# Layer 0 of a four-layer attention network: a set order for TensorE in the two first passes

## The chip, the cores and the metric

The kernel runs on one core of a Trainium2 chip. The metric is the device time of one execution in microseconds (us). In the text DVE is VectorE, ACT is ScalarE, POOL is GpSimd, SP is SyncE, and PE is TensorE; PEld is TensorE's weight load.

## The reference

The network takes x (8 batches, 256 tokens, 320 channels) and a context (8, 120, 192) through four layers. Only layer 0 is touched here. Its attention is quantised: queries, keys and values are rounded to 8-bit integers with one step for the whole tensor, which comes from the largest absolute value in it, and the softmax weights are rounded with a step from the largest weight in the whole tensor.

```
q = fq_sym(x @ Wq); k = fq_sym(ctx @ Wk); v = fq_sym(ctx @ Wv)
scores = einsum('bhnd,bhmd->bhnm', q, k) * dh ** (-0.5)
w = fq_zero(softmax(scores))
out = einsum('bhnm,bhmd->bhnd', w, v)   # then @ Wo + bo
```

with `fq_sym(x) = clip(round(x / d), -128, 127) * d`, `d = max|x| / 127`, and `fq_zero` the same with `d = max(x) / 255`. There are 20 heads of 16 channels. Layer 0 does this twice, first as self attention (keys are the 256 tokens) and then as cross attention (keys are the 120 context tokens), and ends in a feed-forward network. Layers 1 to 3 are attentions and feed-forward networks without rounding.

## The kernel before

Because the steps are maxima over everything, layer 0 goes over all eight batches several times. The class `Quant` (L1180) holds one attention; `s` is the self attention, `c` the cross attention.

*Projections.* `project_all` (L1207) makes queries, keys and values of the self attention batch by batch; ACT copies them from PSUM and `top` (L1201) takes the largest absolute value of each on DVE into a column of `am`. For the last batch the maxima of queries and keys are read from PSUM instead of from the copies. `keys_all` (L1259), `values_all` (L1273) and `queries_all` (L1284) do the same for the cross attention; there, too, the last batch's maxima of queries are read from PSUM, one for each third. `queries_all` has a table `at` of rounds in which a batch is normalised, transposed and projected; the last two batches are pulled together.

*Steps and rounding.* `steps` (L1319) reduces `am` over partitions and makes the steps. `whole(b)` (L1339) rounds: by adding a large number and taking it off again, the queries and keys of batch b become whole numbers in bf16, in five instructions: `tk` (L1347), `tq` (L1350), two halves of the keys (L1353 and L1357), and the queries (L1363 or L1365). They are on POOL, except that with `fast` the keys are on DVE and the last step of the queries is on ACT with a bias tile `magic`. `fast` is used for batch 0 of both attentions and for batch 1 of the cross attention.

*First pass.* It finds the sums of the softmax. A batch has 20 heads in five groups of four. A unit is, for the self attention, one group and half of its heads: 10 units a batch; for the cross attention two groups (or the last one) and half of their heads: 6 units a batch. For a unit there are three kinds of work, with the letters that the prediction uses:

- T, in `tops_all` (L1407): matmuls of the scores with tokens on the partitions (L1422), and a DVE reduction for the largest score of each token (L1425). When a batch is through, three DVE casts and two subtractions split its maxima into bf16 parts (`npx`, L1442 and L1444). In the third unit of the next batch TensorE transposes them (L1433) and ACT copies them to `nTs` (L1436).
- E, in `exps` (L1449): matmuls of the scores with keys on the partitions, and of `sel` with `nTs` to take the maxima off (both L1466), and ACT's exponential (L1473) into a tile `e` of a pool of five.
- S, in `add` inside `sums_all` (L1477): matmuls of `place` with `e` (L1488), which add up the exponentials over keys. When a batch is through, ACT copies its sums (L1493) and DVE takes their smallest (L1494).

T and E each take a pair of PSUM banks from one pool of three pairs, `ps_f`, in turn; so a tile of T or E waits until the reduction or exponential of the tile three before it has read its bank. S uses a pool of two banks, `ps_a`.

*What sets the order.* `weave` (L649) runs several of these generators round by round: in each round every generator whose start has come takes one step. That gives the program order. The order on each engine is then chosen by the framework's scheduler, which may bring an instruction ahead of others of its engine that are not ready in its model; it keeps data dependencies, and manual dependencies where the program adds them. For the self attention the parts are `tops_all` from round 0, `sums_all` (which calls `exps` first and then adds half of the units that wait) from round n + 4 with n = 10, `whole_all` (the rounding of batches 1 to 7) from round 0, and `keys_all` from round 7. The maxima of the cross keys are taken after it by a plain loop. For the cross attention the context's keys and values of later layers are made in the same weave: matmuls at L728, ACT copies to `kst` (L360, L364) and `vst` (L371, L372, L781), and stores to DRAM from SP.

*Second pass.* `weight_steps` (L1514) makes the step of the weights, and `out_all` computes the scores again, rounds the weights, multiplies by the values and projects. For the self attention `queries_all` of the cross attention is woven in from round 8, and three steps of `values_all` from round 5B + 1.

The main part calls these in order: `project_all`, `steps`, `whole(0)`, the weave of the first pass, the second pass, and the same for `c`.

Of the kernel before, what the change touches and what calls it, by code (L numbers as in the profile page):

```python
# [11 lines left out]
F32 = mybir.dt.float32  # L12
# [6 lines left out]
P = 128  # L19
# [35 lines left out]
class Kernel:  # L55
# [118 lines left out]
    def open_quant(self, pool):  # L174
# [8 lines left out]
        self.magic = pool.tile([P, 1], F32, name="magic")  # L183
        nc.gpsimd.memset(self.magic, -MAGIC)
# [94 lines left out]
    def weight_o2(self, pool, name):  # L279
# [8 lines left out]
        return w  # L288

# [274 lines left out]
    def ff_item(self, blk, ln, which, func, w, brow):  # L564
# [11 lines left out]
        def out():  # L576
# [5 lines left out]
            def mm(*args, **kw):  # L582
                nonlocal last
                ins = nc.tensor.matmul(*args, **kw)  # L584
                if last is not None:
                    order = mybir.DependencyInfo(mybir.DependencyClass.NoSync, mybir.DependencyReason.DATA)
                    self.tc.add_manual_dep(ins.ins, last.name, order, reason="order of the rows' forms")
                last = ins.ins
# [591 lines left out]
class Quant:  # L1180
# [5 lines left out]
    def __init__(self, k, pool, kpool, ln, w, brow, cross):  # L1186
# [8 lines left out]
        self.am = pool.tile([P, 3, B + 2], F32, name=f"am_{n}")  # L1195
        nc.gpsimd.memset(self.am, 0.0)
        self.sc = pool.tile([P, 16], F32, name=f"sc_{n}")
        self.q, self.kk, self.v = {}, {}, {}


    def top(self, i, b, src):  # L1201
        self.k.nc.vector.tensor_reduce(
            self.am[: src.shape[0], i, b : b + 1], src, AX.XY if len(src.shape) > 2 else AX.X, ALU.max,
            apply_absolute_value=True,
        )

    def project_all(self):  # L1207
# [11 lines left out]
        for b in range(B):  # L1219
# [29 lines left out]
            if b + 1 < B:  # L1249
                self.top(0, b, q)  # L1250
                self.top(1, b, kt)
                continue

            for i, ps in enumerate((pq, pk)):
                self.top(i, b, ps[:, :, :N])
            for i, ps in enumerate((pq, pk)):
                self.top(i, B, ps[:, i, N:])
# [26 lines left out]
    def queries_all(self):  # L1284
# [12 lines left out]
        def project(b, m):  # L1297
# [3 lines left out]
            if b + 1 == B:  # L1301
                self.top(0, b + m, ps[:, 0, :N])
            elif m == 2:
                self.top(0, b, self.q[b])

        at = {b: [5 * b + i for i in (0, 3, 6, 7, 8)] for b in range(B - 2)}
        at[B - 2] = [5 * B - 10 + i for i in (0, 3, 4, 5, 7)]
        at[B - 1] = [5 * B - 10 + i for i in (3, 6, 7, 8, 9)]  # L1310
        for r in range(5 * B):
            for b in range(B):
                for i, n in enumerate(at[b]):
                    if n == r:
                        norm(b) if i == 0 else turn(b) if i == 1 else project(b, i - 2)
            yield
# [22 lines left out]
    def whole(self, b, fast=False):  # L1339
# [7 lines left out]
        to.tensor_scalar(tk[:, : 3 * nk], kt, sc[:, 7:8], MAGIC, ALU.mult, ALU.add)  # L1347
        yield
        tq = k.work.tile([P, 3 * N], F32, tag="xh", name="tq")
        nc.gpsimd.tensor_scalar(tq, q, sc[:, 6:7], MAGIC, ALU.mult, ALU.add)  # L1350
# [11 lines left out]
        if fast:  # L1362
            nc.scalar.activation(qh.rearrange("p c n -> p (c n)"), tq, AF.Identity, bias=k.magic)  # L1363
        else:
            to.tensor_scalar(qh.rearrange("p c n -> p (c n)"), tq, MAGIC, None, ALU.subtract)  # L1365
# [24 lines left out]
    def whole_all(self):  # L1390

        for b in range(1, B):
            n = 0
            for _ in self.whole(b, self.cross and b == 1):
# [12 lines left out]
    def tops_all(self):  # L1407
# [3 lines left out]
        for b in range(B + 1):  # L1411
            if b < B:
                negm = k.small.tile([P, 4, G, TPB], F32, tag="negm", name="negm")
            for i, (gs, h) in enumerate(self.units):
                if b < B:
                    s = k.pair()
                    for n, g in enumerate(gs):
                        for t in range(TPB):
                            for j in range(2):
                                kt, q = self.operands(b, g, 2 * h + j)  # L1420
                                o = (n * TPB + t) * nk
                                nc.tensor.matmul(  # L1422
                                    s[:, j, o : o + nk], q[:, t * P : (t + 1) * P], kt, start=True, stop=True
                                )
                    nc.vector.tensor_reduce(  # L1425
# [23 lines left out]
    def exps(self, b, gs, heads, kind):  # L1449
# [5 lines left out]
        for shift in (False, True):  # L1455
            for i, g in enumerate(gs):
                for c in range(kc):
                    for at, j in enumerate(heads):
# [7 lines left out]
                        nc.tensor.matmul(  # L1466
# [9 lines left out]

    def sums_all(self):  # L1477

        k, nc, kc, ks = self.k, self.k.nc, self.kc, self.ks
        st, todo = {}, []  # L1480

        def add(b, g, c, es, at):
# [4 lines left out]
            for j in range(4):  # L1487
                nc.tensor.matmul(  # L1488
# [7 lines left out]
        es = []  # L1496
        for b in range(B):
            for gs, h in self.units:

                if h == 0:  # L1500
                    es = []
                    for _ in range(len(todo) - len(self.last) if todo else 0):
                        add(*todo.pop(0))
# [289 lines left out]
```

## Time and profile before

| | us |
|---|---|
| median of three runs | 2235.7 (2229.62 to 2238.51) |
| profiled execution, its own time | 2235.43 |
| profiled execution, span | 2233.4 |
| mean granted clock of TensorE | 0.965 of full speed |
| self projections end, first reduction of the self first pass | 103.9, 111.0 |
| end of the self first pass | about 258 |
| first T of the cross first pass, its end | 414.5, about 547 |

The profile is taken from one execution. Busy times are shares of its span; stretches are read in us from the span's start. The granted clock is the share of full speed that TensorE was allowed. The difference of 2.0 us between the profiled execution's own time and its span lies outside the first and last instruction. The places of the stages are read from the times at which the groups of lines named above begin and end.

### The profile page before, as it was taken

What the parts mean: (1) busy time and instruction counts of PE and PEld (TensorE: products, weight loads), DVE (VectorE), ACT (ScalarE), POOL (GpSimd) and SP (SyncE); (2) the same over time, 40 slices, a digit from 0 to 9 for tenths busy, and PEclk for the clock granted to TensorE, in tenths of its full rate; (3) what the DMA queues carried; (4) which work ended last, traced back from release to release, by engine and by line L of the source; (5) the groups of instructions that cost most, each with busy time, mean ns of one, the idle gap of its engine ahead of it and who ended that gap; (6) DMA issues with size and microseconds to landing.
All of it is one profiled execution on the core that took longest, in us unless ns stands there. A gap on an engine that the chain in (4) does not pass through costs nothing.

```text
span 2233.4 us, 38265 instructions
## 1 busy us (share of the span) xinstructions
PE 2044.5 (92%) x16413; PEld 1201.3 (54%) x16413; DVE 1117.4 (50%) x1698; ACT 825.7 (37%) x1252; POOL 357.9 (16%) x365
## 2 busy tenths in 40 slices
PE   6889878898899999999999999899999799999997
PEld 5643345554444555465555555554555455666664
DVE  4388677555752221335655667611121466556465
ACT  2347878467532121124444443411201233222221
POOL 1092066601411000000000001100000100000100
PEclk9989889898889999999999999999999899999999
DMA  4000000642110000020000001100000201000000
GB/s 117 17 12 2 1 1 4 167 111 57 55 53 28 1 0 1 1 92 2 2 2 22 27 25 35 47 1 0 1 1 2 68 25 32 12 24 26 23 19 16
DMA packets 79303, 63.21 MB, mean 28 GB/s; under 512 B 48410, under 2 KB 68318, under 8 KB 78622
## 3 DMA queue, kind: packets, MB, share of 16 engines
q1 hardware_dynamic: 75070, 57.06, 9.3%
q10 hardware_dynamic: 4064, 3.71, 0.6%
q8 instruction: 129, 2.11, 0.4%
q14 instruction: 40, 0.33, 0.1%
HBM read 42.61 MB, written 17.37 MB: 27 GB/s over the span
## 4 chain that ended last, share of the span: by engine, by line
PE 75%; DVE 16%; ACT 5%; issue 3%; DMA 1%; POOL 1%; SPq 0%; ACTq 0%; DVEq 0%; POOLq 0%
PE pf L120 13%; PE pf L584 13%; PE pf L132 9%; PE pa L120 7%; PE pa L447 6%; PE pf L430 4%; PE pa L584 3%; PE pf L139 3%; PE pf L385 3%; DVE negm L1425 3%; PE pf L1466 3%; PE pf L728 3%; DVE rs L455 2%; PE pa L1488 2%; DVE negm L392 2%
## 5 line engine op out<-in xcount | busy, mean ns | idle before, releaser
L436 ACT ACTIVATE e<-pf 128x1024 f32<-128x1024 f32 (+2 forms) x176 | 158.3, 944 | 234.9 <-PE pf L430 227.8
L392 DVE TENSOR_REDUCE negm<-pf 128x4 f32<-128x1024 f32 (+4 forms) x224 | 188.1, 886 | 108.8 <-PE pf L385 108.8
L584 PE MATMUL pf<-xTf,ff 128*128 128x512 f32 x512 | 232.4, 601 | 5.2 <-DVE negm L392 5.2
L455 DVE RECIPROCAL rs<-pa 128x256 f32<-128x256 f32 x88 | 152.2, 1745 | 144.0 <-PE pa L447 144.0
L477 POOL TENSOR_TENSOR xb<-x_sb,brow 128x640 f32<-128x640 f32 x40 | 62.2, 1555 | 792.2 <-DVE x_sb L483 748.2
L1473 ACT ACTIVATE e<-pf,sc_s 128x1024 f32<-128x1024 f32 x160 | 169.6, 1116 | 49.4 <-PE pf L1466 42.6
L1425 DVE TENSOR_REDUCE negm<-pf 128x4 f32<-128x1024 f32 (+2 forms) x128 | 143.3, 1134 | 68.1 <-PE pf L1422 61.4
L611 DVE SCALAR_TENSOR_TENSOR hT<-pf,cols_sb,gl 128x512 f32<-128x512 f32 x64 | 48.0, 751 | 256.8 <-ACT gl L610 254.5
L120 PE MATMUL pf<-ff,hT 128*128 128x320 f32 x640 | 174.4, 434 | 0.0
L584 PEld LDWEIGHTS pf<-xTf,ff 128*128 128x128 f32 x512 | 94.9, 191 | 125.2 <-issue 119.8
L120 PEld LDWEIGHTS pf<-ff,hT 128*128 128x128 f32 x640 | 120.9, 190 | 55.5 <-issue 6.1
L430 PE MATMUL pf<-qT,kT 32*128 32x256 f32 (+1 forms) x1280 | 122.3, 411 | 21.9 <-DMA qT<-nT 12.8
L610 ACT ACTIVATE gl<-pf,cols_sb 128x512 f32<-128x512 f32 x64 | 43.9, 687 | 248.0 <-PE pf L584 248.0
L385 PE MATMUL pf<-kT,qT 32*128 32x120 f32 (+1 forms) x1920 | 114.8, 329 | 18.3 <-ACT e L436 18.1
L120 PE MATMUL pa<-o,oT 128*128 128x320 f32 x352 | 105.4, 441 | 15.2 <-DVE oT L456 14.1
L385 PEld LDWEIGHTS pf<-kT,qT 32*128 32x128 f32 x1920 | 84.9, 189 | 58.4 <-ACT e L436 27.7
L1466 PE MATMUL pf<-Q,K 32*128 32x256 bf16 (+1 forms) x960 | 90.5, 294 | 25.3 <-DVE negm L1425 13.2
L639 POOL TENSOR_TENSOR xb<-x_sb,brow 128x640 f32<-128x640 f32 x16 | 25.1, 1566 | 543.1 <-DVE x_sb L644 528.7
L447 PE MATMUL pa<-e,v 128*32 128x256 f32 (+1 forms) x1280 | 105.2, 388 | 2.3 <-ACT e L436 1.7
L1581 DVE TENSOR_SCALAR w<-e 128x1024 bf16<-128x1024 f32 (+2 forms) x128 | 87.4, 691 | 37.5 <-ACT e L1473 36.3
L430 PEld LDWEIGHTS pf<-qT,kT 32*128 32x128 f32 (+1 forms) x1280 | 68.7, 183 | 68.3 <-issue 37.3
L132 PE MATMUL pf<-xT,q 128*128 128x256 f32 x384 | 101.0, 392 | 0.4 <-ACT e L436 0.2
(287 smaller groups left out, 3448.1 us busy)
## 6 DMA issues: line engine op xcount, KB each, us to landing
ff<-in_L_xattn_Wff_dram SPq DMA_DIRECT2D x1, 2560.0 KB
qT<-nT SPq DMA_DIRECT2D x160, 4.0 KB
ff<-in_L_xattn_ff_w_dram SPq DMA_DIRECT2D x1, 2560.0 KB
out_dram<-x_sb SPq DMA_DIRECT2D x16, 160.0 KB
kd_cross<-kst SPq DMA_DIRECT2D x8, 300.0 KB
vd_cross<-vst SPq DMA_DIRECT2D x8, 300.0 KB
vd_both<-vst SPq DMA_DIRECT2D x8, 300.0 KB
kT<-kd_cross SPq DMA_DIRECT2D x8, 300.0 KB
```

Of the source, the lines that this page charges most:

```text
L120: self.nc.tensor.matmul(out, l, r, start=i == 0, stop=i == len(pairs) - 1)
L132: self.nc.tensor.matmul(o, *t[c], start=start and c == 0, stop=stop and c == n - 1, skip_group_check=True)
L385: nc.tensor.matmul(s[j // 2][:, j % 2, o : o + nk], qT[r : r + PAD, g, t * P : (t + 1) * P], kT[r : r + PAD, g, :nk], start=True, stop=True,)
L392: nc.vector.tensor_reduce(negm[:, n, 2 * i : 2 * i + 2, g0 : g0 + len(gs), :].rearrange("p j g t -> p j (g t)"), sv[:, :, :, k0:k1], AX.X, ...
L430: nc.tensor.matmul(s[j // 2][:ks, j % 2, o : o + N], kT[r : r + PAD, g, c * ks : (c + 1) * ks], qT[r : r + PAD, g, :], start=True, stop=True,)
L436: nc.scalar.activation(e[:ks, 2 * i : 2 * i + 2, :n], s[i][:ks, :, :n], AF.Exp, scale=scale)
L447: nc.tensor.matmul(o[j * PAD : (j + 1) * PAD, what * N : (what + 1) * N], w, es[g][:ks, j, c * N : (c + 1) * N], start=first and c == 0 an ...
L455: nc.vector.reciprocal(rs, o[:, N:])
L584: ins = nc.tensor.matmul(*args, **kw)
L1425: nc.vector.tensor_reduce(negm[:, 2 * h : 2 * h + 2, gs[0] : gs[-1] + 1, :].rearrange("p j g t -> p j (g t)"), s[:, :, : len(gs) * TPB * n ...
L1466: nc.tensor.matmul(s[at // 2][:ks, at % 2, o : o + N], l, m, start=not shift and o == 0, stop=shift and o + N == n, skip_group_check=True,)
L1473: nc.scalar.activation(e[:ks, :, :n], ps[:ks, :, :n], AF.Exp, scale=self.sc[:ks, 9:10])
```

## The change

It has these parts.

1. A helper `behind` adds a dependency of order alone (no semaphore) between two instructions. `Quant.mm` chains with it all matmuls of T, E and S of an attention's first pass, in program order. The weave names E, T and S as three parts in that order, `exps_all` being split from `sums_all`; S now takes half of the waiting units in even rounds and all in odd ones.
2. In the self attention's weave, `keys_all` starts at round 2 instead of 7; the maxima of the cross keys are ordered behind the reduction of the last T.
3. The last batch's maxima are taken from the SBUF copies, as those of the others are.
4. `whole` with `fast` has `tk` on POOL and `tq`, both halves of the keys and the last step of the queries on DVE; ACT has no part and `magic` goes. Batch 1 of the cross attention is no longer `fast`.
5. `queries_all` has the same rounds for every batch, four more in all; the end of `out_all` has two more rounds and takes one unit from its list in each; the values start three rounds later.

```diff
+    def behind(self, ins, last, reason):
+        if last is not None:
+            order = mybir.DependencyInfo(mybir.DependencyClass.NoSync, mybir.DependencyReason.DATA)
+            self.tc.add_manual_dep(ins.ins, last.ins.name, order, reason=reason)
...
+    def mm(self, *args, **kw):
+        ins = self.k.nc.tensor.matmul(*args, **kw)
+        self.k.behind(ins, self.last_mm, "order of the rows' forms")
+        self.last_mm = ins
...
-            if b + 1 < B:
-                self.top(0, b, q)
-                self.top(1, b, kt)
-                continue
-            for i, ps in enumerate((pq, pk)):
-                self.top(i, b, ps[:, :, :N])
-            for i, ps in enumerate((pq, pk)):
-                self.top(i, B, ps[:, i, N:])
+            self.top(0, b, q)
+            self.top(1, b, kt)
...
-            if b + 1 == B:
-                self.top(0, b + m, ps[:, 0, :N])
-            elif m == 2:
+            if m == 2:
                 self.top(0, b, self.q[b])
-        at = {b: [5 * b + i for i in (0, 3, 6, 7, 8)] for b in range(B - 2)}
-        at[B - 2] = [5 * B - 10 + i for i in (0, 3, 4, 5, 7)]
-        at[B - 1] = [5 * B - 10 + i for i in (3, 6, 7, 8, 9)]
-        for r in range(5 * B):
+        todo = {0: norm, 3: turn, 6: lambda b: project(b, 0), 7: lambda b: project(b, 1), 8: lambda b: project(b, 2)}
+        for r in range(5 * B + 4):
...
-        to.tensor_scalar(tk[:, : 3 * nk], kt, sc[:, 7:8], MAGIC, ALU.mult, ALU.add)
+        nc.gpsimd.tensor_scalar(tk[:, : 3 * nk], kt, sc[:, 7:8], MAGIC, ALU.mult, ALU.add)
...
-        nc.gpsimd.tensor_scalar(tq, q, sc[:, 6:7], MAGIC, ALU.mult, ALU.add)
+        to.tensor_scalar(tq, q, sc[:, 6:7], MAGIC, ALU.mult, ALU.add)
...
-        if fast:
-            nc.scalar.activation(qh.rearrange("p c n -> p (c n)"), tq, AF.Identity, bias=k.magic)
-        else:
-            to.tensor_scalar(qh.rearrange("p c n -> p (c n)"), tq, MAGIC, None, ALU.subtract)
+        to.tensor_scalar(qh.rearrange("p c n -> p (c n)"), tq, MAGIC, None, ALU.subtract)
...
-            for _ in self.whole(b, self.cross and b == 1):
+            for _ in self.whole(b):
...
+    def exps_all(self):
+        self.ready = []
+        for b in range(B):
+            for gs, h in self.units:
+                if h == 0:
+                    self.ready, es = list(self.made) if b or gs[0] else [], []
+                es += self.exps(b, gs, (2 * h, 2 * h + 1), 0, self.mm)[0]
+                if h == 1:
+                    self.made = [(b, g, c, es, i * self.kc + c) for i, g in enumerate(gs) for c in range(self.kc)]
+                yield
+        self.ready += self.made
...
+        for r in range(B * len(self.units)):
+            for _ in range(-(-len(self.ready) // (2 - r % 2))):
+                add(*self.ready.pop(0))
+            yield
+        while self.ready:
+            add(*self.ready.pop(0))
...
-        for r in range(rounds * B + 2):
+        for r in range(rounds * B + 4):
...
-            while len(todo) > (2 if b < B else 0):
+            if len(todo) > (2 if b < B else 0):
                 values(*todo.pop(0))
...
-                if r == rounds * B + 1:
-                    d, left = B, 0
...
-                k.weave((0, s.tops_all()), (n + 4, s.sums_all()), (0, s.whole_all()), (7, c.keys_all()))
+                k.weave(
+                    (n + 4, s.exps_all()), (0, s.tops_all()), (n + 4, s.sums_all()), (0, s.whole_all()), (2, c.keys_all()),
+                )
                 for b in range(B):
-                    c.top(1, b, c.kk[b])
+                    k.behind(c.top(1, b, c.kk[b]), s.last_top, "what is waited for first")
...
-                k.weave((0, s.out_all()), (8, c.queries_all()), (5 * B + 1, islice(v, 3)))
+                k.weave((0, s.out_all()), (8, c.queries_all()), (5 * B + 4, islice(v, 3)))
...
             k.weave(
-                (0, c.tops_all()), (n + 4, c.sums_all()), (0, c.whole_all()), (5, v),
+                (n + 4, c.exps_all()), (0, c.tops_all()), (n + 4, c.sums_all()), (0, c.whole_all()), (5, v),
                 (1, k.paced(islice(ahead, 21), 1)),
             )
```

## The prediction

> **What bounds the kernel now.** I read the page first: the busy shares, the granted clock by slice, the groups.
>
> ```profile
> PE 2044.5 (92%) x16413; PEld 1201.3 (54%) x16413; DVE 1117.4 (50%) x1698; ACT 825.7 (37%) x1252; POOL 357.9 (16%) x365
> ...
> PEclk9989889898889999999999999999999899999999
> ...
> L1473 ACT ACTIVATE e<-pf,sc_s 128x1024 f32<-128x1024 f32 x160 | 169.6, 1116 | 49.4 <-PE pf L1466 42.6
> L1425 DVE TENSOR_REDUCE negm<-pf 128x4 f32<-128x1024 f32 (+2 forms) x128 | 143.3, 1134 | 68.1 <-PE pf L1422 61.4
> ```
>
> TensorE is busy 92% of the span, but a mean over 2233 us says nothing of the changed stages. From the groups by line I placed them: self projections to 106 us, self first pass 111 to 258, self second pass with the cross queries to 410.5, cross first pass 414.5 to 547. All that follows, some 1690 us, is not touched. The third slice of the clock row (112 to 168, the early self pass) has an 8, so the busy time by window comes next (sums of PE, PEld, DVE, ACT, POOL with counts, granted clock, DMA share).
>
> ```profile
> core 0: us, PE busy (x) PEld busy (x) DVE busy (x) ACT busy (x) POOL busy (x), PEclk, DMA share, GB/s
> 111.00:134.00 23.00, 19.32 (x140) 13.92 (x137) 20.23 (x25) 3.29 (x8) 23.00 (x14) 0.72 0.00 1
> 134.00:187.06 53.06, 44.48 (x594) 18.98 (x589) 44.42 (x49) 34.11 (x37) 49.99 (x42) 0.87 0.10 13
> 187.06:231.10 44.04, 40.06 (x606) 16.89 (x606) 39.19 (x49) 34.50 (x37) 0.00 (x0) 1.00 0.01 2
> ...
> 414.50:480.00 65.50, 59.42 (x482) 34.17 (x481) 32.49 (x54) 35.93 (x90) 36.85 (x30) 0.87 0.48 129
> ```
>
> Rows two and three do nearly the same work. While POOL rounds the later batches the stage takes 53.06 us at clock 0.87, once POOL is idle 44.04 at 1.00; in neither is an engine full. So the first pass is a loop of waits. The timeline of one pair of units (start, duration) shows it:
>
> ```profile
> 189.31 0.64 PE L1488 MATMUL pa<-e,place 128*32 128x256 f32 x8
> ...
> 189.88 0.39 PE L1422 MATMUL pf<-K,Q 32*128 32x256 bf16 x4
> ...
> 190.20 0.64 PE L1488 MATMUL pa<-e,place 128*32 128x256 f32 x8
> 190.31 1.23 DVE L1425 TENSOR_REDUCE negm<-pf 128x4 f32<-128x1024 f32 x1 [0.42 <-PE pf L1422]
> ...
> 190.78 0.28 PE L1466 MATMUL pf<-Q,K 32*128 32x256 bf16 x2
> ...
> 190.84 0.28 PE L1422 MATMUL pf<-K,Q 32*128 32x256 bf16 x2
> ...
> 191.59 0.39 PE L1466 MATMUL pf<-Q,K 32*128 32x256 bf16 x4 [0.21 <-DVE negm L1425]
> ```
>
> Call T the largest scores (L1422, 4 matmuls), E the exponentials' scores (L1466, 8), S the sums (L1488). TensorE runs S, T, S, then E and T side by side, waits 0.21 for the DVE reduction that frees E's bank, runs E, and begins again: T starts at 187.06, 189.88, 192.71, so 2.82 a pair and 14.69 us a batch of five pairs. The waits of TensorE over the whole self pass (111 to 258), and over the cross pass (412 to 547), are:
>
> ```profile
> PE pf L1466 <- DVE negm L1425: 12.8, 26, 2.7
> ```
>
> ```profile
> PE pf L1466 <- ACT kst L364: 2.8, 3, 1.9
> ```
>
> Self: 12.8 us in 26 waits of E on a reduction, one of 2.7. Cross: little, and mostly behind ScalarE's context copies.
>
> [...]four T matmuls issue in 0.21 but S follows 0.32 after T's start, so I read 0.11 a switch; E beside T takes 0.60 where E (0.54) after T (0.32) would be 0.86. [...]TensorE idles 2.69 us before 148.51, and S then takes 1.00 to 1.08 instead of 0.57 to 0.64. [...]a cast of npx on DVE takes 0.19 in the third window and 0.86 to 1.55 in the second.
>
> **The change part by part.** I sum against the profiled execution, 2235.43 us (span 2233.4 and 2.0 around it); the median shown is 2235.7, so the forecast stands for both.
>
> *Set order, warm batches.* The order of the built kernel is E, T, S for every unit, in place of S, T, S, (E with T), E for every two. TensorE's own time: E 0.43, T 0.21 + 0.11, S 0.46 + 0.11 is 1.32, twice is 2.64 (the switches rise from 166 to 183 over the pass, which this contains). The loop: the T of a unit takes the bank that the exponential of the unit before it frees, E start to exponential start is 0.70 (182.96 to 183.67), exponential 1.11, signal 0.04, then T 0.32 and S 0.57: 2.74 if it binds over two units. The longer of the two decides: 2.74 against 2.82, five pairs 13.7, plus 0.22 for the transposition, 0.2 for ScalarE's sums (0.47) and 0.1 for the casts, is 14.2. Against 14.69 that is -0.5 a batch, over four warm batches -2. DVE then does 13.1 of 14.2 (39.19/3), so it has slack. Ends: TensorE's own 13.4 (-5) and the old loop, 14.69 (0).
>
> *Set order, early batches.* Their ends, taken at the casts, are 144.69, 163.18, 180.66, 195.5, 210.2: 18.5, 17.5, 14.9, 14.7. The excess of some 7 us is E waiting while DVE's casts crawl beside POOL (idles of 2.69, 1.98, 1.30) and the cold matmuls that follow. The rounding stays on POOL, so the crawl stays; but DVE's reductions now have some 0.5 of slack a pair where they had none, so each of the three idles is 0.5 shorter (-1.5), and half a cold spell goes with them (eight S at 0.45 more is 3.6; half is 1.8): -3. Ends 0 and -6.
>
> *Start of the pass.* Before, keys are rounded on DVE at once (0.62), queries on POOL (1.24) and ScalarE (L1363, 0.93), and the first reduction begins at 111.0. After, POOL rounds the keys (108.1 to 109.3), DVE the queries in two steps, then the two halves of the keys (1.15 and 1.00 beside POOL). The first reduction moves to about 112.0: +1.0 (0.6 to 1.9), on the path, for nothing else is ready. ScalarE's step is saved but is not on it.
>
> *Keys of the cross attention at round 2 in place of 7.* Eight blocks of 6 matmuls (2.9 cold, 1.6 warm) lie at 117.94 to 136, would lie at 113.3 to 131. They move; none is added. T of later units then comes later, DVE's reductions are late before the first E, and the first exponential slips from 134.6 to about 135.9 but with more reductions done. I take +0.4 (-1 to +3; the upper end if TensorE is cold at the first E). *The keys' maxima last:* 8 reductions of 0.53 (4.2 us) move from among the casts to behind the last T. There ScalarE is the bound (exponentials back to back, 2.12 a pair, 236.8 to 255.5), and DVE is idle: cover 14 exponentials, 15 us; 0. Without the cover, up to 2.
>
> *Last maxima from copies.* Self: two reductions of 0.95 for four that sum to 1.95; the first starts after ScalarE's copy either way: 0 (-0.2 to +0.5). Cross: one of 0.95 in place of one of 0.42, but the transposition of the maxima is queued on TensorE behind the context matmuls that end at 410.3: 0; uncovered +0.5. *Queries' schedule* and the drains of the second pass: at 385 to 410.5 TensorE is busy 24.0 of 25.5, the same matmuls in another order: 0 (-1 to +1). *Cross rounding:* batch 0 starts as above, +0.3; batch 1 goes from DVE to POOL, whose round has 13 us to spare: 0.
>
> *Set order, cross pass.* One batch with its context block for the values takes 13.58 (499.38 to 512.96). By hand in the new order: T waits for an exponential that sits behind a copy of vst (0.94) on ScalarE, +0.45; the context matmuls wait for an exponential too, +0.4; E and T no longer side by side, +0.26 twice; less the waits on reductions that go, about -1.0. Net +0.3 a batch, four batches, +1.3 (-2 to +12: with every one of 11 vst copies at 0.5 and four kst copies of 2.1 us at 1.6 in the way). What queues behind the order: every T, E and S, as each stands behind the one before.[...]
>
> Sum: -2 - 3 + 1.0 + 0.4 + 0.3 + 1.3 = -2.0. 2235.4 - 2.0 is 2233.4; I say 2233.
>
> **The rivals.** A repeat resolves about 0.5% of this kernel, 11 us, so faster means under 2224.5 and slower over 2246.9.
>
> *The order dissolves the stalls.* The slack of DVE absorbs POOL's stretches and the cold spells go: early batches at 15.0 instead of 18.5 and 17.5 (-6), warm at 13.4 (-5), cross at 0, start +1.4, so -9.6; with the cross waits on reductions and kst gone too (2.3 + 2.8), about -14: 2221. For: no engine is full in any of the windows, and the two early intervals are 6.6 longer than two warm ones. Against: casts and sums on DVE still stand ahead of a reduction, and a fixed order can't slip other work in.
>
> *Slower: ScalarE's copies inside a fixed order.* In the cross pass T of a unit waits for its predecessor's exponential, and that one for a kst copy (2.1) or vst copy (0.94) ahead of it. Before, TensorE took a T or an S that was ready; now it waits. Price as above: 11 x 0.5 + 4 x 1.6 = 12, with the start 1.7 and no gain in self: 2249. It decides from the point at which the cross pass is over 12 us longer than 132.5. For: 2.8 us of waits behind kst already, ScalarE busy 55% to 64% there. Against: two banks of slack between T and E.
>
> *All given back.* TensorE has no shorter loop, because E of two units on waits for the reduction as it does now: self 0, start +1.4, cross +1.3: 2238. *The order isn't changed at all* can be excluded: the built kernel's list of TensorE instructions has E, T, S throughout.
>
> **How the numbers follow.** The forecast 0.40 (2228 to 2240 around 2233), given back 0.23, together within 0.5%; between forecast and faster rival, still within, 0.05; the faster rival 0.20, the slower 0.12. Faster 0.20, within 0.68, slower 0.12. To leave out no more than 2 in 10 the range goes to the edge of the faster rival, 2221, and to 2246, leaving out the slower one and the far end of the faster.
>
> **What would show it.** Right: T starts 2.7 to 2.75 apart a pair in the warm batches, E waiting on reductions nearly gone from the waits; first reduction near 112; first window's cast intervals some 1 to 2 shorter; the cross pass at 133 to 134. Wrong: E still waiting 0.2 a pair; the idles of 2 to 3 us before 187 gone altogether, or a clock of 1.00 from 140 on (faster rival); ScalarE's kst and vst named as what T and E wait for, over 10 us in sum (slower rival). What would upset it most is the clock[...].

## The result and the profile after

The changed kernel takes 2305.1 us (median of four runs, 2300.1 to 2319.7), the kernel before 2235.0 in the same comparison: a ratio of 1.0334, interval 1.0305 to 1.0363. It is 70 us slower. The profiled execution has a span of 2298.3 us, 64.9 more than before. The page of after, the lines that answer to those shown of before:

```profile
PE 2124.9 (92%) x16413; PEld 1230.3 (54%) x16413; DVE 1123.8 (49%) x1693; ACT 825.9 (36%) x1249; POOL 363.7 (16%) x368
...
PEclk9965558999888999999999999999999999999999
...
L1464 ACT ACTIVATE e<-pf,sc_s 128x1024 f32<-128x1024 f32 x160 | 173.2, 1113 | 114.2 <-PE pf L1205 92.3
...
L1416 DVE TENSOR_REDUCE negm<-pf 128x4 f32<-128x1024 f32 (+2 forms) x128 | 144.7, 1136 | 112.7 <-PE pf L1205 112.5
```

TensorE runs the same 16413 matmuls and is busy 80 us longer. The exponentials and the reductions take as long as before (1113 and 1136 ns), but their engines sit idle ahead of them for 114 and 113 us, mostly for TensorE, where it was 49 and 68. The clock row tells why: four slices in a row read 6 5 5 5. The stages, from the DVE reductions that close each of them:

| us | before | after | difference |
|---|---|---|---|
| self projections | 105.9 | 103.6 | -2.3 |
| self first pass, with its start | 151.8 | 219.4 | +67.6 |
| self second pass, cross queries | 151.2 | 152.6 | +1.4 |
| cross first pass, with its start | 137.4 | 134.4 | -3.0 |
| the rest | 1687.1 | 1688.3 | +1.2 |

The loss lies in the self first pass alone; the prediction's parts for it add up to some 4 us less, and it takes 67.6 us more. Its windows (busy time of PE, PEld, DVE, ACT, POOL, then the granted clock):

```profile
111.00:131.00 20.00, 18.23 (x141) 14.54 (x141) 13.80 (x17) 3.66 (x8) 20.00 (x12) 0.87 0.10 12
131.00:187.00 56.00, 53.77 (x452) 21.45 (x453) 36.74 (x37) 27.35 (x28) 50.86 (x43) 0.52 0.06 8
187.00:231.00 44.00, 44.00 (x368) 17.02 (x366) 24.32 (x30) 21.05 (x21) 0.00 (x0) 0.50 0.00 1
231.00:322.00 91.00, 91.00 (x754) 33.34 (x752) 38.14 (x53) 46.01 (x47) 0.00 (x0) 0.50 0.00 1
```

From about 133 us on TensorE is granted half its clock, and it doesn't get the other half back before the pass is all but over (321 us), although from 187 to 322 it is busy in every microsecond. In the window 187 to 231 it gets through 368 matmuls; before, 606. The timeline of TensorE where the clock falls:

```profile
128.48 0.39 PE L1205 MATMUL pf<-K,Q 32*128 32x256 bf16 x4 [0.21 <-ACT K L1271]
129.58 0.39 PE L1205 MATMUL pf<-K,Q 32*128 32x256 bf16 x4 [0.70 <-DVE negm L1416]
130.82 0.26 PE L1205 MATMUL pf<-Q,K 32*128 32x256 bf16 x1 [0.85 <-DVE negm L1416]
...
133.36 0.61 PE L1205 MATMUL pf<-Q,K 32*128 32x256 bf16 x4 [0.92 <-ACT e L1464]
```

and some 54 us later, with POOL done:

```profile
186.86 0.61 PE L1205 MATMUL pf<-Q,K 32*128 32x256 bf16 x4
187.26 0.64 PE L1205 MATMUL pf<-nTs,sel 32*128 32x256 bf16 x4
187.68 0.63 PE L1205 MATMUL pf<-K,Q 32*128 32x256 bf16 x4
188.25 1.08 PE L1205 MATMUL pa<-e,place 128*32 128x256 f32 x8
189.26 0.60 PE L1205 MATMUL pf<-Q,K 32*128 32x256 bf16 x4
```

Four waits that sum to 2.7 us out of some 5 stand ahead of the half clock; none is longer than 0.92. At half clock a unit takes 2.40 us (186.86 to 189.26: E 0.82, T 0.57, S 1.01), and no wait shows. E and T come one after the other: by the 14 rounds between them the T after an E is of the same half of the heads, that is of the same row groups, and it starts 0.82 us after the E (186.86, 187.68). In the order of before the T after an E was of the other half and started 0.03 us after it at half clock (152.37, 152.40), 0.06 at full clock (190.78, 190.84).

### The profile page after: what moved, and what is told of

It reads as the page before. It is cut to its first block, busy times and chain, and to the rows that moved or that the text cites. A ratio compares the mean times of both kernels' runs of the same rounds, so it can differ in the third digit from the quotient of the medians.

```text
span 2298.3 us, 38261 instructions
## 1 busy us (share of the span) xinstructions
PE 2124.9 (92%) x16413; PEld 1230.3 (54%) x16413; DVE 1123.8 (49%) x1693; ACT 825.9 (36%) x1249; POOL 363.7 (16%) x368
## 4 chain that ended last, share of the span: by engine, by line
PE 77%; DVE 13%; ACT 5%; issue 3%; SPq 2%; POOL 1%; DMA 1%; ACTq 0%; DVEq 0%; POOLq 0%
PE pf L120 13%; PE pf L588 12%; PE pf L132 9%; PE pa L120 6%; PE pa L451 6%; PE pf L1205 5%; PE pa L1205 4%; PE pf L434 4%; PE pa L588 3%; PE pf L139 3%; PE pf L389 3%; DVE rs L459 2%; PE pf L730 2%; DVE negm L396 2%; DVE rs L1119 2%
## 5 line engine op out<-in xcount | busy, mean ns | idle before, releaser
L1464 ACT ACTIVATE e<-pf,sc_s 128x1024 f32<-128x1024 f32 x160 | 173.2, 1113 | 114.2 <-PE pf L1205 92.3
L1416 DVE TENSOR_REDUCE negm<-pf 128x4 f32<-128x1024 f32 (+2 forms) x128 | 144.7, 1136 | 112.7 <-PE pf L1205 112.5
L120 PE MATMUL pa<-o,oT 128*128 128x320 f32 x352 | 107.2, 446 | 15.2 <-DVE oT L460 14.1
L1205 PE MATMUL pa<-e,place 128*32 128x256 f32 (+1 forms) x960 | 114.1, 551 | 1.0 <-ACT e L1464 0.9
L1464 ACT ACTIVATE e<-pf,sc_c 120x1024 f32<-120x1024 f32 (+1 forms) x96 | 90.2, 982 | 30.2 <-PE pf L1457 25.4
```

The costliest lines, as they stand in the source:

```text
L120: self.nc.tensor.matmul(out, l, r, start=i == 0, stop=i == len(pairs) - 1)
L1205: ins = self.k.nc.tensor.matmul(*args, **kw)
L1416: self.last_top = nc.vector.tensor_reduce(negm[:, 2 * h : 2 * h + 2, gs[0] : gs[-1] + 1, :].rearrange("p j g t -> p j (g t)"), s[:, :, : l ...
L1464: nc.scalar.activation(e[:ks, :, :n], ps[:ks, :, :n], AF.Exp, scale=self.sc[:ks, 9:10])
```

## The experiments

All ratios are against the kernel before, run on the same chip. The theory from here on is called the trap: in the set order a unit at half clock leaves so much of the array unused that the clock is not given back, whatever first took it. Its rivals are the early keys, the order itself at any clock, and the other parts of the change.

**1. The keys from round 7 again.**

```diff
-(2, c.keys_all()),
+(7, c.keys_all()),
```

> The changed kernel with the cross keys from round 7 again, all else as changed. Trap theory (the set order, once TensorE is at half clock, keeps it there, and the early keys only opened the door): the pass falls into half clock later, at one of the stalls beside POOL, or at the first exponentials all the same; 2250 to 2305 us, and from the fall on the cycle of a unit is 2.40 us with no recovery before the sums' tail. Early-keys theory (only the start with the keys at round 2 costs): clock 1.00 through the warm batches, self first pass as before, 2235 us or a little less.

Measured 2311.1 us, ratio 1.0353 (1.0325 to 1.0382). That is 6 us above the range of either theory. The clock is at 0.50 from about 145 to 313 us: it falls some 12 us later and stays as low. The early keys are not the cause; the clock falls without them too.

**2. A burst of dense matmuls while the clock is at half.**

```diff
+    def burst(self, count):
+        for _ in range(count):
+            ps = self.k.pair()
+            for i in range(2):
+                self.mm(ps[:, i, :C], self.k.ident, self.k.x[:, i, :], start=True, stop=True)
+        yield
...
+(40, s.burst(6)),
```

> The changed kernel with twelve extra matmuls of 128x128 by 320 in fp32 (their result is not used) in the chain at round 40 of the self first pass, when TensorE is at half clock; they take 5 to 13 us. Trap theory: the dense burst brings the clock to 1.00, and as the order runs at 2.7 to 2.8 us a pair when warm, it stays there for the rest of the pass or until the next long stall: 2245 to 2275 us. Theory that this order can't be held at full clock whatever: clock back at 0.5 within some 10 us of the burst, 2310 to 2318 us.

Measured 2264.9 us, ratio 1.0141 (1.0104 to 1.0178): a kernel with more work is 40 us faster than the changed one. The timeline of TensorE around the burst, and the windows ahead of it and behind it:

```profile
196.32 0.63 PE L1205 MATMUL pf<-K,Q 32*128 32x256 bf16 x4
196.88 1.08 PE L1205 MATMUL pa<-e,place 128*32 128x256 f32 x8
197.90 7.75 PE L1205 MATMUL pf<-x_sb,ident 128*128 128x320 f32 x24
205.58 0.39 PE L1205 MATMUL pf<-Q,K 32*128 32x256 bf16 x4
205.81 0.38 PE L1205 MATMUL pf<-nTs,sel 32*128 32x256 bf16 x4
206.02 0.38 PE L1205 MATMUL pf<-K,Q 32*128 32x256 bf16 x4
206.33 0.64 PE L1205 MATMUL pa<-e,place 128*32 128x256 f32 x8
```

```profile
187.00:197.90 10.90, 10.90 (x93) 3.95 (x89) 6.59 (x9) 5.58 (x5) 0.00 (x0) 0.50 0.01 2
205.65:245.00 39.35, 39.28 (x566) 19.06 (x566) 35.34 (x41) 32.24 (x34) 0.00 (x0) 1.00 0.01 2
```

The same four groups take 2.40 us a unit ahead of the burst and about 1.38 behind it. The clock is back some 2 us into the burst (0.50 in the microsecond from 199, 1.00 in that from 200) and stays at 1.00 to the end of the pass. So the order can be held at full clock; in the self first pass it did not climb back to it.

**3. T beside E again, by one round.**

```diff
-(n + 4, s.exps_all()), (0, s.tops_all()), (n + 4, s.sums_all()),
+(n + 5, s.exps_all()), (0, s.tops_all()), (n + 5, s.sums_all()),
```

> The changed kernel with exponentials and sums of the self first pass one round later, so that the T after an E is of the other half of the heads and can run beside it; matmuls and chain are the same. If TensorE stays at half clock because E and T no longer overlap (too thin an activity), this recovers: 2230 to 2245 us and a pair of units near 2.6 to 2.8 us. If what matters is that the two S of a pair no longer stand close together, nothing changes: 2295 to 2310 us at clock 0.5.

Measured 2243.0 us, ratio 1.0058 (1.0035 to 1.0081). The self first pass takes 152.0 us, as before (151.8). The clock falls here too, after waits of 2.96 and 2.27 us, but it comes back within 3 to 7 us:

```profile
168.27 1.08 PE L1205 MATMUL pa<-e,place 128*32 128x256 f32 x8
169.28 0.61 PE L1205 MATMUL pf<-Q,K 32*128 32x256 bf16 x4
169.60 0.40 PE L1205 MATMUL pf<-K,Q 32*128 32x256 bf16 x2
169.68 0.42 PE L1205 MATMUL pf<-nTs,sel 32*128 32x256 bf16 x2
...
170.24 0.86 PE L1205 MATMUL pa<-e,place 128*32 128x256 f32 x8
171.04 0.39 PE L1205 MATMUL pf<-Q,K 32*128 32x256 bf16 x4
```

T starts among the matmuls of E, 0.32 us after it, the unit at half clock takes 1.97 us instead of 2.40, and S (0.80 to the next start instead of 1.01) is where the clock returns. The median is still some 11 us over the kernel before. In the profile, one of the faster runs, the cross pass takes 146.3 us, 9 more than before, with the clock at half from about 461 to 481.

**4. The kernel before with the keys from round 2.**

```diff
-(7, c.keys_all())
+(2, c.keys_all())
```

> The kernel before with one number changed: the cross keys from round 2. Trap theory: it falls to half clock at about the same place as the changed kernel, but recovers within some 10 to 15 us as the kernel before does elsewhere: 2233 to 2245 us. Early-keys theory: most of the 70 us is here too, 2290 to 2305 us.

Measured 2228.1 us, ratio 0.9985 (0.9966 to 1.0004), under the range of either theory. It falls to half clock at about the same place (0.54 over 130 to 140), is back at 145, falls again and is back by 156. The early keys cost nothing that can be measured here.

**5. More work that fills the array: S twice.**

```diff
+            for j in range(0 if self.cross else 4):
+                self.mm(
+                    ps[j * PAD : (j + 1) * PAD, N : 2 * N], k.place[:ks, g, :],
+                    es[j // 2][:ks, j % 2, at * N : (at + 1) * N],
+                    start=False, stop=end, skip_group_check=True,
+                )
```

> The changed kernel with every S of the self first pass done twice, the second time into an unused half of its bank (320 more fp32 matmuls in the trace's four column tiles; nothing reads them). More work on the engine that is the bound. If TensorE stays at half clock because too little of the array works (E and T use half of the rows' groups, S all of it), the doubled S lifts the share of the whole array in a cycle from some 0.63 to some 0.73, the clock recovers, and the kernel with more work is faster than the changed one: 2260 to 2285 us, a unit near 1.78 us. If the share isn't what counts, the unit takes 3.3 us at half clock: 2370 to 2390 us.

Measured 2271.5 us, ratio 1.0192 (1.0150 to 1.0235), 34 us faster than the changed kernel. But the clock did not return at once. It stayed at half for some 45 us in an even beat of 3.26 us a unit, and came back in the middle of an S:

```profile
176.27 1.94 PE L1205 MATMUL pa<-e,place 128*32 128x256 f32 x16
178.14 0.60 PE L1205 MATMUL pf<-Q,K 32*128 32x256 bf16 x4
178.54 0.63 PE L1205 MATMUL pf<-nTs,sel 32*128 32x256 bf16 x4
178.97 0.63 PE L1205 MATMUL pf<-K,Q 32*128 32x256 bf16 x4
179.53 1.27 PE L1205 MATMUL pa<-e,place 128*32 128x256 f32 x16
180.73 0.39 PE L1205 MATMUL pf<-Q,K 32*128 32x256 bf16 x4
```

**6. More work that leaves the array half empty: T twice.**

```diff
+                                for _ in range(1 if self.cross else 2):
+                                    self.mm(s[:, j, o : o + nk], q[:, t * P : (t + 1) * P], kt, start=True, stop=True)
```

> The changed kernel with every T of the self first pass done twice (same operands, same result; the second half runs in the same row groups). TensorE is busy for a larger part of the time than in the changed kernel, but the share of the whole array falls to some 0.61. Array-share theory: still at half clock, a unit 2.8 us, 2330 to 2345 us. If it is the share of time with matmuls in flight that counts: the clock recovers, 2245 to 2265 us.

Measured 2338.4 us, ratio 1.0477 (1.0433 to 1.0522). Half clock to the end of the pass (248.0 us), a unit 2.83 us, in which TensorE has no idle time:

```profile
190.00:230.00 40.00, 40.00 (x344) 17.35 (x340) 18.96 (x21) 16.97 (x18) 0.00 (x0) 0.50 0.00 1
```

Experiments 5 and 6 both add busy time, and TensorE has no idle time in either (38.00 us busy of 38.00 from 140 to 178 in experiment 5, 40.00 of 40.00 here); the one brings the clock back and the other doesn't. So in these runs the time in which TensorE has matmuls under way doesn't decide alone.

**7. The offset in both passes.** The edit of experiment 3, and in the cross attention's weave:

```diff
-(n + 4, c.exps_all()), (0, c.tops_all()), (n + 4, c.sums_all()),
+(n + 5, c.exps_all()), (0, c.tops_all()), (n + 5, c.sums_all()),
```

> The changed kernel with exponentials and sums one round later in both first passes, so that T runs beside E in the cross pass too. If the 9 us that the offset in the self pass alone still lost came from the cross pass at half clock in the same way: clock 1.00 there but for the start, cross pass 134 to 138 us, 2228 to 2238 us. If they came from the fixed order itself: as with the self offset alone, 2240 to 2248 us.

Measured 2237.3 us, ratio 1.0027 (1.0013 to 1.0040). The total came where the first branch put it, but its profile has 143.2 us in the cross pass, not 134 to 138. The gain over experiment 3 is 6 us; that it comes from the clock in the cross pass is not shown.

**8. The set order alone, on the kernel before.** `behind`, `Quant.mm`, `exps_all` and `sums_all` of the change, and:

```diff
-k.weave((0, s.tops_all()), (n + 4, s.sums_all()), (0, s.whole_all()), (7, c.keys_all()))
+k.weave((n + 4, s.exps_all()), (0, s.tops_all()), (n + 4, s.sums_all()), (0, s.whole_all()), (7, c.keys_all()))
```

> The kernel before with the set order alone, in both first passes; keys from round 7, last maxima, rounding of batch 0, queries' rounds as before. Trap theory: all of the loss is here, 2295 to 2315 us, self first pass some 65 us longer at clock 0.5. If another part of the change does it (the rounding of batch 0 or the maxima), it stays at 2230 to 2245 us.

Measured 2295.6 us, ratio 1.0329 (1.0252 to 1.0407), from 2278 to 2322: all of the loss, within its interval. Its profile is of the fastest run; there the self first pass takes 193.6 us, 42 more than before, and ran at full clock until E waited for a reduction that stood behind a cast of 2.15 us beside POOL:

```profile
172.11 0.64 PE L1209 MATMUL pa<-e,place 128*32 128x256 f32 x8
174.82 0.39 PE L1209 MATMUL pf<-Q,K 32*128 32x256 bf16 x4 [2.07 <-DVE negm L1439]
...
175.85 1.08 PE L1209 MATMUL pa<-e,place 128*32 128x256 f32 x8
176.87 0.60 PE L1209 MATMUL pf<-Q,K 32*128 32x256 bf16 x4
```

Behind this wait of 2.07 us the clock is at half from about 175.5 to 295, 3 us ahead of the end of the pass. That the longer runs are those in which an earlier wait brought the clock down would fit, but they left no trace.

**9. Filling with bf16 instead of fp32.**

```diff
+            for j in range(0 if self.cross else 6):
+                self.mm(
+                    ps[:, N : 2 * N], k.ident16, k.sel[:, 0, :2, :].rearrange("p g n -> p (g n)"),
+                    start=False, stop=end, skip_group_check=True,
+                )
```

> The changed kernel with six extra bf16 matmuls of 128x128 by 256 behind every S of the self first pass, into an unused half of its bank (nothing reads them). It asks whether it was S's fp32 or the whole array that let the doubled S recover. Whole-array theory: the clock recovers within some 10 us of the start of the sums; a unit then takes about 2.06 us warm, 2275 to 2300 us with a clock of 1.00 for most of the self first pass. fp32 theory: half clock to the end of the pass, a unit of 3.8 us, 2400 to 2430 us.

Measured 2292.4 us, ratio 1.0270 (1.0239 to 1.0301): less than the changed kernel, with 480 matmuls of 128x128 more. The windows before and after the second filled unit:

```profile
131.00:142.00 11.00, 8.93 (x72) 3.90 (x71) 7.55 (x8) 4.72 (x5) 11.00 (x7) 0.59 0.32 40
143.40:170.00 26.60, 26.60 (x335) 14.67 (x336) 18.17 (x19) 14.78 (x15) 26.60 (x17) 1.00 0.01 2
```

The clock fell once more in this pass, at 177 behind a wait, and was back at 187. So more bf16 work ended the half clock too, within some 10 us; it does not take more fp32.

**10 to 12. Towards a version that keeps what is good.** The order alone with the offset in both passes (10), the changed kernel with both offsets and keys from round 7 (11), and the changed kernel without its set order (12: `sums_all` of before, no chain).

```diff
# 10, on the kernel of experiment 8, in both weaves
-(n + 4, s.exps_all()), (0, s.tops_all()), (n + 4, s.sums_all()),
+(n + 5, s.exps_all()), (0, s.tops_all()), (n + 5, s.sums_all()),
# 11, on the kernel of experiment 7
-(2, c.keys_all()),
+(7, c.keys_all()),
# 12, on the changed kernel, in both weaves
-(n + 4, s.exps_all()), (0, s.tops_all()), (n + 4, s.sums_all()),
+(0, s.tops_all()), (n + 4, s.sums_all()),
```

> The kernel before with the set order alone, exponentials and sums one round later in both passes (T beside E), keys from round 7. Trap theory: short spells at half clock, self first pass 148 to 152 us, 2222 to 2235 us. If the order costs time even with T beside E: 2236 to 2245 us.

> The changed kernel with both offsets and the keys from round 7. Against the one with both offsets and keys from round 2 (2237 us) it tells what the early keys are worth in that order: if the early keys leave TensorE without dense work at the first exponentials, this is 3 to 8 us faster, 2229 to 2234 us; if they save time as they seemed to in the order of before, it is 2 to 5 us slower, 2239 to 2242 us.

> The changed kernel without its set order: order of T, E and S, and the scheduler's freedom, as before; keys from round 2, their maxima last, maxima from copies, rounding of batch 0 on POOL and DVE, queries' rounds as changed. If the loss is the order's alone: 2225 to 2238 us, no half clock of over 15 us in the first passes. If other parts cost some of it, 2240 us or more.

Measured 2232.4 us (ratio 1.0000, 0.9983 to 1.0017), 2234.8 (1.0013, 0.9991 to 1.0034) and 2226.1 (0.9982, 0.9963 to 1.0001). Experiment 12 closes the account: the parts of the change other than the order cost nothing. (Its longest spell at half clock, over the 15 us that it was expected to stay under, is at the start of the cross pass, some 24 us; before it is 17.) Experiment 11 lies between the ranges of its two theories. Experiments 7 and 11 do not differ by more than their intervals, so the early keys are worth nothing there either. In the profile of 10 the self first pass takes 146.1 us, 6 less than before, and the cross pass 145.2, 8 more.

**13. The order with the offset in the self pass alone**, on the kernel before; the cross pass as before.

```diff
# on the kernel of experiment 10, in the cross weave
-(n + 5, c.exps_all()), (0, c.tops_all()), (n + 5, c.sums_all()),
+(0, c.tops_all()), (n + 4, c.sums_all()),   # sums_all of before, no chain
```

> The kernel before with the set order, one round later for exponentials and sums, in the self first pass only; cross pass and all else as before. The order with the offset in both passes had a self first pass of 146.1 us (before: 151.8) and a cross pass of 145.2 (before: 137.4). If what the set order loses in the cross pass is the order's own, this keeps the one and not the other: 2222 to 2229 us, under the kernel before. If the cross pass's length is only where the clock happens to fall: 2229 to 2236 us.

Measured 2223.6 us, the kernel before 2226.2 on the same chip: ratio 0.9990 (0.9975 to 1.0004). In its profile the self first pass takes 145.9 us (before 151.8) and the cross pass 137.6, as the first branch says, but against the kernel beside it the gain isn't clear of the interval. Inconclusive. No version is clearly faster than the kernel before.

**14 and 15. A mean or a dense stretch.** Experiment 9 with two matmuls instead of six, and experiment 5 for every second S.

```diff
# 14
-            for j in range(0 if self.cross else 6):
+            for j in range(0 if self.cross else 2):
# 15
-            for j in range(0 if self.cross else 4):
+            for j in range(0 if self.cross or (g * kc + c) % 2 else 4):
```

> The fill of bf16 matmuls with two instead of six behind every S of the self first pass: 1.01 + 0.5 of some 2.90 us at half clock fill the array, a share of 0.52, between the changed kernel (0.42, no recovery) and S twice (0.57, after 45 us). [...]half clock to the end of the pass, 2340 to 2350 us. [...]it recovers, 2250 to 2275 us.

> S twice in every second unit only: mean share 2.88 of 5.66 us at half clock, 0.51, nearly that of the two-matmul fill, but in an uneven beat[...]. If the mean share decides, this does what the two-matmul fill does (both recover or both stay). If one dense window is enough, it recovers within some 10 to 20 us, 2250 to 2262 us, whatever the fill does; if it stays at half clock, 2335 to 2345 us.

Measured 2348.2 us (ratio 1.0484, 1.0417 to 1.0550) and 2263.2 (1.0142, 1.0093 to 1.0190). In the profiles the even fill stays at half clock for some 195 us, until the T have come to an end, and the uneven S gets out within 8 us. Both profiles are of the fastest of three runs: the others of 15 took 2263 and 2266 us against its 2243 and had a lower mean clock (0.960 and 0.956 against 0.968), so the clock may have come back later there; those of 14 took 2348 and 2354 against 2319 (0.918 and 0.917 against 0.933). First the fill: its window, one cycle of 2.95 us, and the place where the clock comes back, behind the last T; then the uneven S where the clock returns:

```profile
200.00:290.00 90.00, 90.00 (x672) 32.70 (x668) 41.39 (x49) 35.60 (x36) 0.00 (x0) 0.50 0.00 1
```

```profile
249.89 1.08 PE L1205 MATMUL pa<-e,place 128*32 128x256 f32 x8
250.91 0.61 PE L1205 MATMUL pa<-sel,ident 128*128 128x256 bf16 x2
251.44 0.61 PE L1205 MATMUL pf<-Q,K 32*128 32x256 bf16 x4
...
252.84 1.08 PE L1205 MATMUL pa<-e,place 128*32 128x256 f32 x8
...
326.73 1.08 PE L1205 MATMUL pa<-e,place 128*32 128x256 f32 x8
...
329.25 1.08 PE L1205 MATMUL pa<-e,place 128*32 128x256 f32 x8
330.26 0.39 PE L1205 MATMUL pa<-sel,ident 128*128 128x256 bf16 x2
```

```profile
137.85 1.94 PE L1205 MATMUL pa<-e,place 128*32 128x256 f32 x16
139.72 0.61 PE L1205 MATMUL pf<-Q,K 32*128 32x256 bf16 x4
...
141.11 0.89 PE L1205 MATMUL pa<-e,place 128*32 128x256 f32 x8
141.93 0.39 PE L1205 MATMUL pf<-Q,K 32*128 32x256 bf16 x4
```

At half clock the array is filled for 1.55 of 2.95 us in the one (0.53) and for 2.88 of 5.66 in the other (0.51). So the mean share over a cycle doesn't decide alone. Nor does the length of a dense piece: behind the last T (323.6) the even fill is still in pieces of 1.55 us, but they come every 2.52 us, and the clock is back at 330.

## Why the prediction was wrong, point by point

**The step that failed** is the set order's, warm and early batches alike: it took the unit's time at full clock, 1.32 of TensorE's own, as what the whole pass would run at, and priced a fall of the clock as a spell ("half a cold spell", a whole one being 3.6 us) that ends by itself. That a busy TensorE gets its clock back was the author's estimate. In the early self pass of the kernel before the clock did come back while TensorE was busy (at half until about 154.4 behind the wait that ends at 148.51, and from 168.1 to 171.5 behind the one that ends at 166.62); in the changed one TensorE was busy without a break for 135 us at half clock, so there the measurement goes against it. The price of a fall was thus not 3.6 us but 1.0 us for every unit until the end of the pass: 2.40 instead of 1.41 (half of 2.82), times some 75 units. For the order in the self pass the sum had -2 - 3; the pass took 67.6 us longer.

**The evidence was in the price of the overlap.** The prediction read E beside T as 0.60 instead of 0.86 and charged it as time (0.26 in the cross pass; in the self pass it is inside the 1.32). It was worth more at half clock: there the kernel before puts its pair in 3.99 us (149.48 to 151.35 and 151.35 to 153.79, less 0.32 for the transposition), the changed one in 4.80.

**The warm loop** was right. Behind the burst of experiment 2 two units take 2.77 us (S at 209.32 and 212.09), a batch 14.1 (casts at 233.15 and 247.26), and waits on reductions are gone; forecast were 2.74 and 14.2. The kernel never came to run in it.

**The early batches** were wrong in sign: the waits beside POOL remained (2.07, 2.27, 2.96 us in experiments 8 and 3), and half clock followed on each. The reading that in the early windows no engine is full left out POOL, which is busy for 23.00 of 23.00 and 49.99 of 53.06 us in the first two.

**The start** was right: from the reduction of the steps to the first T's reduction 5.9 us after (103.6 to 109.54), 5.1 before; +0.8 against +1.0.

**Start, keys, maxima, queries' rounds, rounding**: forecast +1.7 in sum. Experiment 12 has them all, at 0.9982 (0.9963 to 1.0001), that is -4 us with an interval of -8 to 0. What was given for the upper end of the keys, half clock at the first E, came close in the changed kernel: the first E (130.82) is still at full clock, the second (133.36) at half. Experiment 1 shows the same a little later with the keys at round 7.

**The cross pass**: forecast +1.3, its profile -3.0. That number says little. With the same order there the profiles of other experiments lie between 133.3 and 152.5 us (14 and 1), and they are the longer the more of the pass is at half clock: by its mean clock some 8 us in the changed kernel and in 14, 58 and 54 in the two longest (1 and 2). With the order of before they lie between 137.4 and 141.5. The clock falls there too and comes back each time, in 1 only after 36 us.

**The slower rival** named ScalarE's copies. In the changed cross pass they hold T and E for 3.2 us in sum (2.7 behind kst, 0.5 behind vst), not 12. Right side, wrong mechanism. **All given back** and **the faster rival** fell with the clock.

**What stays open** is what brings the clock back. The kernels at half clock, worked out from the starts in the timeline of one execution each (filled: S, a fill, or E beside T with 0.43 us for the T; E or T alone, on half of the row groups, is counted as nothing, which is a choice):

| kernel | longest dense piece, us | filled, us of us | share | clock comes back |
|---|---|---|---|---|
| T twice | 1.01 | 1.01 of 2.83 | 0.36 | no, to the end of the pass |
| changed | 1.01 | 1.01 of 2.40 | 0.42 | no, 165 us |
| the same behind the last T | 1.01 | 1.01 of 1.98 | 0.51 | no, 20 us |
| two bf16 behind S | 1.55 | 1.55 of 2.95 | 0.53 | no, some 190 us |
| the same behind the last T | 1.55 | 1.55 of 2.52 | 0.62 | within 7 us |
| every second S twice | 1.87 | 2.88 of 5.66 | 0.51 | within 8 us |
| S twice | 1.87 | 1.87 of 3.26 | 0.57 | after some 45 us |
| six bf16 behind S | 2.41 | 2.41 of 3.80 | 0.63 | within some 10 us |
| before | 1.02, and E beside T | 2.46 of 3.99 | 0.62 | within some 6 us |
| offset | 1.01, and E beside T | 1.44 of 1.97 | 0.73 | within 3 to 7 us |

Neither column sorts the rows alone: at a share of 0.51 to 0.53 the clock came back in one row and not in two, with pieces of 1.55 us in one and not in the other. From 0.57 up it came back in every row. That doesn't carry over to other work. In the cross pass of experiment 1 the clock stayed at half from 525 to 561, with context matmuls in between, some on all rows and some on half of them. In the lines here, which merge both kinds, an S (on 120 rows) and the first context matmuls (on all 128) make one dense piece of some 2.7 us (540.50 to about 543.2), and the clock stayed at half:

```profile
540.50 1.08 PE L1205 MATMUL pa<-e,place 120*32 120x256 f32 x8
541.51 4.43 PE L730 MATMUL pf<-ctxT,ck 128*128 128x208 f32 x12
545.87 0.68 PE L1205 MATMUL pf<-Q,K 32*120 32x256 bf16 x4
```

Why S twice took some 45 us in an even beat of 3.26 before its clock came back, what decides whether a clock comes back, and why the clock fell after waits of so different a length (none over 0.92 us in the changed kernel, 2.07 to 2.96 in experiments 8 and 3), was not shown.

## What to carry to other kernels

When a loop's matmuls use a part of the array, work out its cycle at half clock as well as at full clock (here 2.40 us a unit against about 1.38), and compare what it fills with the rows of the table. A cycle like one that stayed at half clock (1.01 us filled of 2.40, 165 us) is a reason for doubt; a loop that runs well only until something stalls it is worth what it does at half clock. Spells of half clock in the profile of before that end by themselves are a warning: look for what ends them (here E beside T: in experiment 3 the clock was back within 3 to 7 us) ahead of any reordering. And a busy share near 100% is no sign of health: read it with the granted clock beside it (91.00 us busy of 91.00 at 0.50).

## What the runs showed of the hardware that was not expected

Waits that sum to 2.7 us in some 5, none over 0.92 (changed kernel), and elsewhere a single wait of 2.07 us (experiment 8), were followed by half clock. In the changed kernel a TensorE that was busy in every microsecond stayed at half clock for 135 us and, with two short breaks (0.26 and 0.91), for 188; in experiment 2 the first 2 us of a burst of 12 dense matmuls (24 in the trace) ended it. Work that nobody reads made the kernel some 14 to 43 us faster than the changed one, by their ratios (experiments 9, 5, 2 and 15).
